# Attention on four quarter arrays: 64x64 tiles for scores and contexts, and the denominators in the score ring

## The chip, the cores and the metric

The kernel runs on one core of a Trainium2 chip. The metric is the device time of one execution in microseconds, the median of three runs. The engines meant below are TensorE (matrix products into PSUM, which has eight banks of 128 partitions x 512 float32), VectorE, ScalarE, GpSimd (POOL) and SyncE (SP, which issues DMAs).

## The reference

Two layers follow each other, all in float32. The first is attention over an image of 1024 channels and 32x32 pixels, so 1024 tokens, for four images. The second is a bottleneck of convolutions (1x1, 3x3, 1x1) with batch norms and a residual. The change touches only the attention:

```python
qkv = (x @ w_qkv.T + b_qkv).reshape(B, N, 3, nh, hd)      # nh 16 heads of hd 64, N 1024 tokens
q, k, v = (qkv[:, :, 0], qkv[:, :, 1], qkv[:, :, 2])
q = _rmsnorm(_apply_rope(q, cos, sin)); k = _rmsnorm(_apply_rope(k, cos, sin))
scores = jnp.einsum('bqhd,bkhd->bhqk', q, k) * hd ** (-0.5)
attn = jax.nn.softmax(scores, axis=-1)
ctx = jnp.einsum('bhqk,bkhd->bqhd', attn, v).reshape(B, N, inner)
out = _rmsnorm(ctx @ w_proj.T, norm_out_w) + residual
```

## The kernel before, in words

For each of the four images (b) the kernel projects q, k and v (`project2`, a Strassen-Winograd scheme of two levels), runs attention, and projects the contexts (y). Products with weights are cut so that TensorE works on 128x128 weights.

Attention (`attention`, L767) runs once for each half c of the queries (512 of them) and in it over eight pairs of heads hp. So an image has 16 pairs to go through, and the four images 64. In one pair:

- **Scores.** The 1024 keys are cut in eight blocks t of 128. For each block L787 makes two products, one for each head j of the pair. A head's 64 channels lie in one half of the partitions, so each product uses 64 rows and 128 columns of the array: two row tiles. Both go into a tile of two PSUM banks of the ring `sc`, which has three such tiles.
- **Probabilities.** ScalarE takes the exponential of both banks at once (L794) into `probs_`, which holds one pair's eight blocks.
- **Sums.** VectorE adds the blocks' probabilities into `d_` (L798, L800): seven additions of 128x1024 elements.
- **Contexts.** L808 multiplies the probabilities with v, 128 keys by the 64 channels of one head: two column tiles of 128x64, accumulated over the eight blocks in one PSUM bank, `cx`. ScalarE copies it to `q_all` (L813), over the queries, which are no longer needed.
- **Denominators.** After each second pair L841 sums `d_` over the partitions with a matrix of ones, as four column tiles of 128x32, into the bank `dn`. In the first half of the queries of images 1 to 3 (`fold`) GpSimd's DMAs fold four pairs' sums first, and one product for four pairs, `sum_of_eight` (L857), takes its place, also into `dn`. It is called two pairs later, between the scores and the contexts (L802). ScalarE copies `dn` at once (L863), or at the head of the next pair (`inverses`, L885, called by `late`); the copy goes to memory and back so that the reciprocal has few elements in a row, and `mean_of_v` (L761) multiplies the contexts some pairs later. For the last two pairs of an image there is no next pair: VectorE takes the reciprocal of `dn` itself (L891), after the y projection has begun.
- **What else is done in a pair**, after the contexts: `mean_of_v`; one waiting step (`next_waiting`), such as one head pair's rope of k (`turn`); and `extra` steps, in image 0 sums of weight blocks for the other projections (L392 to L395, L409 to L412), in the second half of image 3 the sums of the filters (L1086 to L1091).

`psum_for` (L189) closes PSUM's pools and opens those of the next stage: `o1` and `o2`, four banks each, for projections; `sc`, `cx` and `dn` for attention. Pools lie in PSUM in the order in which they are opened, and a tile of a new pool waits for the tile of the old pool that lay in the same bank (`reuse_waits="tile"`). In the y projection after attention, `start(0)` takes the first `o1` tile, `second(0)` the first `o2` tile, and VectorE forms four sums (`inner`, L450 to L454) before the reciprocal.

TensorE, VectorE, ScalarE and GpSimd are scheduled by hand here: each works its instructions off in the order in which the program issues them.

Of the kernel before, what the change touches and what calls it, by code (L numbers as in the profile page):

```python
# [13 lines left out]
ALU = mybir.AluOpType  # L14
# [4 lines left out]
P = 128  # L19
B, C, H, W = 4, 1024, 32, 32  # L20
N = H * W
NT = C // P
HD = 64
NHP = C // (2 * HD)
CH = 512
# [60 lines left out]
def program(ctx, tc, x, wblk, w2, w3, vecs, cos, sin, out, bad):  # L86


    nc = tc.nc
# [68 lines left out]
    with tc.tile_pool(name=f"st{u}", bufs=2) as st, ExitStack() as s:  # L158
# [30 lines left out]
        def psum_for(stage):  # L189

            open_pools.close()
            psum.clear()
            sizes = {
                "proj": [("o1", [P, CH], 4), ("o2", [P, CH], 4)],
                "att": [("sc", [P, 2, CH], 3), ("cx", [P, CH], 1), ("dn", [P, CH], 1)],
            }[stage]
            for name, shape, bufs in sizes:
                pool = open_pools.enter_context(
                    tc.tile_pool(name=f"{name}{u}{nc.next_id()}", bufs=bufs, space=PSUM, reuse_waits="tile")
                )  # L200
                psum[name] = (pool, shape)

        def bank(kind, name):
            pool, shape = psum[kind]
            return pool.tile(shape, F32, tag=kind, name=name)

        def temp(name):
            return tmp.tile([P, CH], F32, tag="tmp", name=name)
# [58 lines left out]
        def next_waiting():  # L267
            cost, step = waiting.popleft()
            spend(cost)
            step()  # L270
# [471 lines left out]
        def shifts(q_all, k_all, n, hp, c):  # L742

            rows = []
            for j in range(2):
                d = slice(j * HD, (j + 1) * HD)
                row = temp(f"row_{n}_{j}")[0:1, :]
                for t in range(CH // P):
                    sc = bank("sc", f"sm_{n}_{j}_{t}")
                    q = q_all[d, hp, c * CH + t * P : c * CH + (t + 1) * P]  # L750
                    for kh in range(N // CH):
                        nc.tensor.matmul(sc[:, kh], q, k_all[d, hp, half[kh]], start=True, stop=True)
                    m = acc.tile([P, 1], F32, tag="m", name=f"m_{n}_{j}_{t}")
                    nc.vector.tensor_reduce(m, sc.rearrange("p a k -> p (a k)"), AX.X, ALU.max, negate=True)
                    o = bank("dn", f"mt_{n}_{j}_{t}")
                    nc.tensor.matmul(o[0:1, :P], m, ident, start=True, stop=True)
                    nc.vector.tensor_copy(row[:, t * P : (t + 1) * P], o[0:1, :P])
                rows.append(row)
            return rows
# [7 lines left out]
        def attention(b, c, q_all, k_all, v, probs_, late, ready, extra, slow, steps_in_all, load_parts, fold):  # L767


            at = half[c]  # L770
            sums_ = []
            for hp in range(NHP):
                n = f"{b}_{c}_{hp}"
                if late:
                    late.pop(0)()
                rows = shifts(q_all, k_all, n, hp, c) if bad is None else None
                probs = []
                if fold and hp % 2 == 0:
                    d_ = fold[hp // 4][:, hp % 4 // 2 * 2 : hp % 4 // 2 * 2 + 2, :]
                else:  # L780
                    d_ = acc.tile([P, 2, CH], F32, tag="tot", name=f"den_{n}")
                for t in range(N // P):
                    p = probs_[:, t]
                    sc = bank("sc", f"sc_{n}_{t}")
                    for j in range(2):
                        d = slice(j * HD, (j + 1) * HD)
                        nc.tensor.matmul(  # L787
                            sc[:, j], k_all[d, hp, t * P : (t + 1) * P], q_all[d, hp, at],
                            start=True, stop=bad is not None,
                        )  # L790
                    if bad is None:
                        for j in range(2):
                            nc.tensor.matmul(sc[:, j], ones[0:1, :], rows[j], start=False, stop=True)
                    nc.scalar.activation(p, sc, AF.Exp)  # L794
                    if t == 3:
                        load_parts()
                    if t == 1:
                        nc.vector.tensor_tensor(d_, probs[0], p, ALU.add)  # L798
                    elif t > 1:
                        nc.vector.tensor_tensor(d_, d_, p, ALU.add)  # L800
                    probs.append(p)
                if eights and eights[0][0] <= c * NHP + hp:  # L802
                    eights.pop(0)[1]()
                o = bank("cx", f"cx_{n}")
                for t in range(N // P):
                    for j in range(2):
                        h0 = (2 * hp + j) * HD
                        nc.tensor.matmul(  # L808
                            o[j * HD : (j + 1) * HD, :], v[:, t, h0 : h0 + HD], probs[t][:, j],
                            start=(t == 0), stop=(t == N // P - 1),  # L810
                        )

                nc.scalar.copy(q_all[:, hp, at], o)  # L813
                sums_.append(d_)
                if hp % 2 == 1:
                    for r in ready:
                        mean_of_v(q_all, *r)
                    ready.clear()
                if fold:
                    halve(hp, d_, fold[hp // 4][:, hp % 4 // 2 * 2 : hp % 4 // 2 * 2 + 2, :])  # L820
                    if hp % 4 == 3:
                        eights.append((hp + 2, lambda n=n, hp=hp: sum_of_eight(b, n, hp, fold[hp // 4], ready)))
                if half_done and half_done[0][0] <= c * NHP + hp:
                    half_done.pop(0)[1]()
                if slow:
                    slow.pop(0)()

                if waiting:
                    next_waiting()
                slots = NCH * NHP - 1  # L830
                if extra and steps_in_all == 0 and hp > 0:
                    extra.pop(0)()
                for _ in range(len(extra) - -(-steps_in_all * max(slots - 1 - c * NHP - hp, 0) // slots) if steps_in_all else 0):
                    extra.pop(0)()
                if hp % 2 == 0 or fold:
                    continue
                dn = bank("dn", f"dn_{n}")
                for i, d_ in enumerate(sums_):
                    for j in range(2):
                        q = slice((2 * i + j) * QH, (2 * i + j + 1) * QH)  # L840
                        nc.tensor.matmul(dn[q, :], ones[:, :QH], d_[:, j], start=True, stop=True)  # L841
                sums_ = []
                late.append(lambda *a, n=n, hp=hp, dn=dn: inverses(b, c, hp, n, dn, ready))

        half_done, eights = [], []
        low, high = slice(0, P // 2), slice(P // 2, P)
# [9 lines left out]

        def sum_of_eight(b, n, hp, home, ready):  # L857

            dn = bank("dn", f"dn_{n}")
            for i in range(4):  # L860
                nc.tensor.matmul(dn[i * QH : (i + 1) * QH, :], halves, home[:, i, :], start=True, stop=True)
            r = temp(f"rec_{n}")
            nc.scalar.copy(r, dn)  # L863
            k = 2 * b * NCH * NHP + 2 * (hp - 3)
            few, rows = to_few(n, k, 8, r[:: QH // 2, :])

            def invert():
                nc.vector.reciprocal(few, few)
                nc.sync.dma_start(rows, few)
                for i in range(2):  # L870

                    at = [dens[k + 4 * i + q, :].partition_broadcast(QH) for q in (0, 2, 1, 3)]
                    spread(0, hp - 2 + 2 * i, n + f"_{i}", ready, at)

            half_done.append((hp + 3, invert))
# [288 lines left out]
        for b in range(B):  # L1164
            units = units_of(room)
            q_all = kv.tile([P, NT, N], F32, tag="q", name=f"q_{b}")
# [16 lines left out]
            k_all = kp.tile([P, NT, N], F32, tag="k", name=f"k_{b}")  # L1183
# [10 lines left out]
            v = room  # L1194
# [15 lines left out]
            def load_parts():  # L1210

                while todo and len(made) < 2:
                    made.append(todo.pop(0)(pieces, nc.sync))
# [279 lines left out]
        for b in range(B):  # L1493
# [34 lines left out]
            if b == 0 and bad is not None:  # L1528
                o = ps.tile([P, CH], F32, tag="mm", name="fit")
# [20 lines left out]
        for f in range(NT):  # L1550
# [8 lines left out]
            for i, k in order:  # L1559
                b, c = divmod(i, NCH)  # L1560
                nc.tensor.matmul(  # L1561
                    os[i], w3t[k][f // NH][:, f % NH, :], h2[b, k][:, half[c]],
                    start=(k == 0), stop=(k == NPT - 1),
# [11 lines left out]
            sc, sh = norms[f] = norm_of(stats, col("g3", f), col("be3", f), f"3_{f}")  # L1575
# [81 lines left out]
```

## Time and profile before

| | |
|---|---|
| time before, median of three runs | 2673.18 us (2672.54 to 2675.76) |
| profiled execution, first to last instruction (span) | 2669.7 us |
| median less span | 3.5 us |
| TensorE busy | 2643.4 us (99%) |
| VectorE busy | 2112.1 us (79%) |
| ScalarE busy | 1111.9 us (42%) |
| attention of images 0, 1, 2, 3, TensorE's stretches | 233.5, 230.4, 230.3, 230.9 us |
| mean granted TensorE clock | 0.998 |

The profiled execution's own time is taken as its span and the 3.5 us around it. A line of the page's groups gives the source line, the engine, the operation, the tiles written and read, the shape and the count; then busy time and mean duration in ns; then the engine's idle time before these instructions and what ended it. For a matmul, 64*128 means 64 rows and 128 columns of the array. Every float32 product is two matmuls, each with a weight load of its own (PEld). A line of a timeline gives start, duration, engine, source line, tiles, shape and count, and in brackets the idle time before it. A line of a table by stretches gives the stretch, its length, and busy time and instructions of TensorE, its weight loads, VectorE, ScalarE and GpSimd.

### The profile page before, as it was taken

How to read it: one execution, taken by the hardware profiler on the slowest of the kernel's cores; microseconds unless marked ns; L12 is line 12 of the kernel's file. 1: busy time of each engine (PE TensorE's matmuls, PEld its weight loads, DVE VectorE, ACT ScalarE, POOL GpSimd, SP SyncE). 2: the span in 40 equal slices, each digit the busy share in tenths (PEclk: the TensorE clock that was granted, in tenths of full speed). 3: DMA queues.
4: the chain of work that ended last, by engine and by line, in shares of the span. 5: the costliest groups of instructions: out<-in, count | busy, mean ns of one | idle time of the engine just before them, and what ended most of it. 6: DMA issues, size and time to landing. Idle time of an engine off the chain costs nothing.

```text
span 2669.7 us, 32558 instructions
## 1 busy us (share of the span) xinstructions
PE 2643.4 (99%) x11338; PEld 1650.7 (62%) x11338; DVE 2112.1 (79%) x2538; ACT 1111.9 (42%) x1549; POOL 470.6 (18%) x573
## 2 busy tenths in 40 slices
PE   9999999999999999999999999999999999999997
PEld 4448533488888333688886333888884335846843
DVE  5668899988787866788879667887988679877987
ACT  2222465423442555433343555233425654312266
POOL 2542233301011221200111222100111222010000
PEclk9999999999999999999999999999999999999999
DMA  7887676767667451456775541665774443583165
GB/s 277 292 255 215 197 244 206 236 211 250 169 181 215 83 102 41 157 152 222 191 196 148 92 77 33 211 203 178 191 214 87 82 100 115 172 279 103 64 236 206
DMA packets 255627, 459.22 MB, mean 172 GB/s; under 512 B 34912, under 2 KB 127632, under 8 KB 255456
## 3 DMA queue, kind: packets, MB, share of 16 engines
q1 hardware_dynamic: 210528, 306.73, 36.6%
q0 software_dynamic: 44928, 150.33, 22.3%
q8 instruction: 93, 1.52, 0.2%
q14 instruction: 78, 0.64, 0.1%
HBM read 327.43 MB, written 97.01 MB: 159 GB/s over the span
## 4 chain that ended last, share of the span: by engine, by line
PE 93%; DMA 3%; DVE 2%; issue 1%; ACT 1%; POOL 0%; SPq 0%; DVEq 0%; POOLq 0%; ACTq 0%
PE sc L787 16%; PE cx L808 16%; PE p_v L480 12%; PE p_y L485 12%; PE p_k L485 10%; PE p_q L485 9%; PE c L1561 4%; PE pa_q L303 2%; PE c2x L1422 2%; PE c L989 2%; PE c2y L1422 2%; PE pa_k L303 1%; PE c L948 1%; PE pc_q L303 1%; PE c1s L989 1%
## 5 line engine op out<-in xcount | busy, mean ns | idle before, releaser
L794 ACT ACTIVATE p<-sc 128x1024 f32<-128x1024 f32 x512 | 476.3, 1043 | 26.4 <-PE sc L787 24.3
L787 PE MATMUL sc<-q,k 64*128 64x512 f32 x2048 | 457.7, 596 | 0.0
L800 DVE TENSOR_TENSOR den<-den,p 128x1024 f32<-128x1024 f32 x312 | 384.9, 1234 | 33.6 <-DVE den L800 1.4
L787 PEld LDWEIGHTS sc<-q,k 64*128 64x128 f32 x2048 | 189.9, 186 | 265.2 <-issue 121.6
L808 PE MATMUL cx<-p,to 128*64 128x512 f32 x1536 | 340.2, 595 | 0.0
L808 PEld LDWEIGHTS cx<-p,to 128*64 128x64 f32 x1536 | 106.0, 137 | 228.7 <-issue 228.7
L480 PE MATMUL p_v<-w_v,x 128*128 128x256 f32 x928 | 209.9, 379 | 0.0
L485 PE MATMUL p_y<-q,w_y 128*128 128x256 f32 x928 | 209.8, 379 | 0.0
L765 POOL TENSOR_SCALAR q<-q,vec 128x512 f32<-128x512 f32 x64 | 128.1, 2010 | 384.7 <-DVE q L764 376.5
L485 PEld LDWEIGHTS p_y<-q,w_y 128*128 128x128 f32 x928 | 176.0, 190 | 27.1 <-issue 3.4
L480 PEld LDWEIGHTS p_v<-w_v,x 128*128 128x128 f32 x928 | 176.1, 190 | 25.2 <-DVE x L451 0.9
L813 ACT COPY q<-cx 128x512 f32<-128x512 f32 x64 | 37.6, 587 | 360.0 <-PE cx L808 360.0
L798 DVE TENSOR_TENSOR den<-p 128x1024 f32<-128x1024 f32 x52 | 64.6, 1243 | 120.4 <-ACT p L794 120.4
L485 PE MATMUL p_q<-to,w_q 128*128 128x256 f32 x672 | 152.2, 379 | 0.0
L485 PE MATMUL p_k<-to,w_k 128*128 128x256 f32 x672 | 152.2, 379 | 0.0
L485 PEld LDWEIGHTS p_q<-to,w_q 128*128 128x128 f32 x672 | 127.4, 190 | 18.4 <-issue 1.2
L485 PEld LDWEIGHTS p_k<-to,w_k 128*128 128x128 f32 x672 | 127.4, 190 | 18.4 <-issue 1.2
L808 PE MATMUL cx<-p,rq 128*64 128x512 f32 x512 | 113.4, 595 | 0.0
L1561 PE MATMUL c<-h,w 128*128 128x512 f32 x256 | 110.3, 592 | 0.5 <-ACT h L1464 0.5
L800 DVE TENSOR_TENSOR den_T<-den_T,p 128x1024 f32<-128x1024 f32 x72 | 88.2, 1225 | 7.5
L727 POOL DMA_DIRECT2D k<-ks x64 | 57.9, 1097 | 190.7 <-ACT p L794 71.1
L485 PE MATMUL p_y<-to,w_y 128*128 128x256 f32 x384 | 90.4, 380 | 1.1 <-DMA w_y<-wdf 1.0
(490 smaller groups left out, 4266.0 us busy)
## 6 DMA issues: line engine op xcount, KB each, us to landing
w_v<-wd2f SPq DMA_DIRECT2D x112, 256.0 KB, 3.2
w_y<-wd2f SPq DMA_DIRECT2D x112, 256.0 KB, 2.8
w_q<-wd2f SPq DMA_DIRECT2D x84, 256.0 KB, 2.8
w_k<-wd2f SPq DMA_DIRECT2D x84, 256.0 KB, 2.6
wd2f<-w_pre POOLq DMA_DIRECT2D x68, 256.0 KB, 3.9
x<-in_x_dram SPq DMA_DIRECT2D x64, 256.0 KB, 5.9
q<-qs POOLq DMA_DIRECT2D x64, 256.0 KB, 5.5
k<-ks POOLq DMA_DIRECT2D x64, 256.0 KB, 4.5
```

The source lines that it names most:

```text
L303: nc.tensor.matmul(o, w[:, i, :], r(i), start=first and i == 0, stop=last and i == NH - 1, skip_group_check=True,)
L480: nc.tensor.matmul(o[:, q].rearrange("p (g f) -> p g f", g=2), r[:, i, q * P : (q + 1) * P], wt[:, :, i, :], skip_group_check=True, **at,)
L485: nc.tensor.matmul(o[:, q], wt[:, q, i, :], r[:, i, :], skip_group_check=True, **at)
L765: nc.gpsimd.tensor_scalar(cx, cx, col("bv", hp), None, ALU.add)
L787: nc.tensor.matmul(sc[:, j], k_all[d, hp, t * P : (t + 1) * P], q_all[d, hp, at], start=True, stop=bad is not None,)
L794: nc.scalar.activation(p, sc, AF.Exp)
L798: nc.vector.tensor_tensor(d_, probs[0], p, ALU.add)
L800: nc.vector.tensor_tensor(d_, d_, p, ALU.add)
L808: nc.tensor.matmul(o[j * HD : (j + 1) * HD, :], v[:, t, h0 : h0 + HD], probs[t][:, j], start=(t == 0), stop=(t == N // P - 1),)
L989: nc.tensor.matmul(o, wt[:, i, :], rows(i), start=first and i == 0, stop=last and i == NH - 1, skip_group_check=True,)
L1422: nc.tensor.matmul(o[:, r * TR * TC : (r + 1) * TR * TC], uw[2 * h + r, j][:, i * PL + f * P : i * PL + (f + 1) * P], vt[b, i][:, 2 * h + ...
L1561: nc.tensor.matmul(os[i], w3t[k][f // NH][:, f % NH, :], h2[b, k][:, half[c]], start=(k == 0), stop=(k == NPT - 1),)
```

## The change

Scores are made by four products a block instead of two: the 128 keys are cut in two halves, so each product uses a tile of 64 rows and 64 columns. Contexts are made by four products a block as well: the 128 keys are cut in two halves of the partitions, each half accumulates in a PSUM bank of its own, and `cx` has two banks. ScalarE copies the first as before; VectorE adds the second to it, after the pair's other steps. The pool `dn` is gone: denominators take half of a tile of the ring `sc`. The call of `sum_of_eight` moves from between scores and contexts to behind that addition.

```diff
-                "att": [("sc", [P, 2, CH], 3), ("cx", [P, CH], 1), ("dn", [P, CH], 1)],
+                "att": [("sc", [P, 2, CH], 3), ("cx", [P, 2, CH], 1)],
...
-            sums_ = []
+            sums_, contexts = [], []
...
-                    for j in range(2):
-                        d = slice(j * HD, (j + 1) * HD)
-                        nc.tensor.matmul(
-                            sc[:, j], k_all[d, hp, t * P : (t + 1) * P], q_all[d, hp, at],
-                            start=True, stop=bad is not None,
-                        )
+                    for keys in (low, high):
+                        for j, d in enumerate((low, high)):
+                            nc.tensor.matmul(
+                                sc[keys, j], k_all[d, hp, t * P + keys.start : t * P + keys.stop], q_all[d, hp, at],
+                                start=True, stop=bad is not None,
+                            )
...
-                if eights and eights[0][0] <= c * NHP + hp:
-                    eights.pop(0)[1]()
                 o = bank("cx", f"cx_{n}")
                 for t in range(N // P):
                     for j in range(2):
                         h0 = (2 * hp + j) * HD
-                        nc.tensor.matmul(
-                            o[j * HD : (j + 1) * HD, :], v[:, t, h0 : h0 + HD], probs[t][:, j],
-                            start=(t == 0), stop=(t == N // P - 1),
-                        )
-
-                nc.scalar.copy(q_all[:, hp, at], o)
+                        for i, keys in enumerate((low, high)):
+                            nc.tensor.matmul(
+                                o[j * HD : (j + 1) * HD, i], v[keys, t, h0 : h0 + HD], probs[t][keys, j],
+                                start=(t == 0), stop=(t == N // P - 1),
+                            )
+
+                nc.scalar.copy(q_all[:, hp, at], o[:, 0])
+                contexts.append((q_all[:, hp, at], o[:, 1]))
...
+                for cx, other in contexts:
+                    nc.vector.tensor_tensor(cx, cx, other, ALU.add)
+                contexts.clear()
+                if eights and eights[0][0] <= c * NHP + hp:
+                    eights.pop(0)[1]()
                 if hp % 2 == 0 or fold:
                     continue
-                dn = bank("dn", f"dn_{n}")
+                dn = bank("sc", f"dn_{n}")[:, 0]
...
         def sum_of_eight(b, n, hp, home, ready):
-            dn = bank("dn", f"dn_{n}")
+            dn = bank("sc", f"dn_{n}")[:, 0]
```

The second program (`bad is None`), which runs only where a denominator leaves its bounds, gets the same tiles; it does not run on these inputs.

More of the change, by code (lines that the diff above doesn't have):

```diff
@@ L754, in shifts @@
                     nc.vector.tensor_reduce(m, sc.rearrange("p a k -> p (a k)"), AX.X, ALU.max, negate=True)
-                    o = bank("dn", f"mt_{n}_{j}_{t}")
+                    o = bank("sc", f"mt_{n}_{j}_{t}")[:, 0]
                     nc.tensor.matmul(o[0:1, :P], m, ident, start=True, stop=True)
```

## The prediction

> **What bounds the kernel now.** I read the page's busy line and chain first, then its groups, then the waits, then TensorE's and VectorE's timelines of attention.
>
> ```profile
> PE 2643.4 (99%) x11338; PEld 1650.7 (62%) x11338; DVE 2112.1 (79%) x2538; ACT 1111.9 (42%) x1549; POOL 470.6 (18%) x573
> ...
> PE 93%; DMA 3%; DVE 2%; issue 1%; ACT 1%; POOL 0%; SPq 0%; DVEq 0%; POOLq 0%; ACTq 0%
> PE sc L787 16%; PE cx L808 16%; PE p_v L480 12%; PE p_y L485 12%; PE p_k L485 10%; PE p_q L485 9%; PE c L1561 4%; PE pa_q L303 2%; PE c2x L1422 2%; PE c L989 2%; PE c2y L1422 2%; PE pa_k L303 1%; PE c L948 1%; PE pc_q L303 1%; PE c1s L989 1%
> ...
> L787 PE MATMUL sc<-q,k 64*128 64x512 f32 x2048 | 457.7, 596 | 0.0
> L800 DVE TENSOR_TENSOR den<-den,p 128x1024 f32<-128x1024 f32 x312 | 384.9, 1234 | 33.6 <-DVE den L800 1.4
> ```
>
> TensorE is the path: scores and contexts are 16% each. 2048 score matmuls of 596 ns would be 1221 us in a row, but the chain gives them 427: two row tiles run side by side. So both products already fill the array. The timeline of TensorE over one pair of heads, then a denominator:
>
> ```profile
> 907.59 0.60 PE L808 MATMUL cx<-p,to 128*64 128x512 f32 x2
> 908.12 7.14 PE L787 MATMUL sc<-q,k 64*128 64x512 f32 x32
> 915.19 7.09 PE L808 MATMUL cx<-p,to 128*64 128x512 f32 x32
> 922.21 1.13 PE L787 MATMUL sc<-q,k 64*128 64x512 f32 x4
> ...
> 346.12 1.06 PE L841 MATMUL dn<-den,ones 128*32 128x512 f32 x8
> ```
>
> A pair of heads takes 922.21 - 908.12 = 14.09 us. By the single start times, matmuls start two at a time (6 ns apart, one per tile) every 0.429 us; only at the changes of shape is it more: 0.519 and then 0.480 from scores to contexts (0.141 over), 0.529 and then 0.534 from contexts to scores (0.205 over). 32 x 0.429 = 13.73 and 0.346 make the 14.08. The last line shows four column tiles at once: eight matmuls in 1.06 us.
>
> VectorE, by stretch (attention of images 0 and 1), and the end of image 0's attention:
>
> ```profile
> 287.60:521.10 233.50, 233.43 (x1081) 84.21 (x1080) 213.13 (x223) 133.24 (x151) 76.41 (x105) 1.00 0.67 217
> 865.80:1096.20 230.40, 230.40 (x1065) 83.76 (x1064) 165.07 (x145) 131.85 (x149) 51.32 (x48) 1.00 0.35 69
> ...
> 521.11 1.06 PE L841 MATMUL dn<-den,ones 128*32 128x512 f32 x8
> 522.11 3.72 PE L485 MATMUL p_y<-q,w_y 128*128 128x256 f32 x16
> 525.01 3.35 DVE L891 RECIPROCAL rec<-dn 128x512 f32<-128x512 f32 x1
> 528.41 0.92 PE L485 MATMUL p_y<-y,w_y 128*128 128x256 f32 x3 [0.86 <-DVE rec L891]
> ```
>
> VectorE is busy 213 of 233.5 us in image 0, and between its 223 instructions lie some 0.06 to 0.1 us each: it has almost no slack there, 65 us in image 1. And the last line is what I build on: a PSUM bank makes the next stage wait. The last denominator sits in the `dn` bank until the 3.35 us reciprocal has read it, and the output projection, whose second `o2` tile is that bank (7), waits.
>
> [...] 0.141 and 0.205 us at each change of shape, nothing at a change of tile. [...] The forecast takes the drain's size and VectorE's load from the trace.
>
> **The change, part by part.**
>
> *Four 64x64 tiles.* Twice the matmuls, a quarter of the array each. The trace shows two row tiles at once (scores), two and four column tiles at once, not two by two. If four run, a step stays 0.429 us and the stream costs nothing more or less. Weight loads (137 ns for 64 columns, 187 for 128) stay under it. Bounds: nothing, and twice the time if only two run (rival 2). I take nothing.
>
> *No change of shape.* A pair of heads without a denominator goes from 14.08 to 13.73. One with a denominator keeps two changes (64x64 to 128x32 and back), so it only saves scores to contexts: 15.08 to 14.94. In images 1 to 3: eleven pairs x 0.346, the one with both sums at its end (pair 9 of 16) 0.29, three with one sum and the last pair 0.14 each: 4.65 us an image.
>
> *The added VectorE instruction.* 128x512 from SBUF and PSUM: 64 of them. The nearest row, the projection's addition from PSUM (L506), has 0.685 us, with a pitch of 0.61 back to back; I take 0.65, bounds 0.61 and 0.72. It stands behind all of a pair's VectorE work (sums of exponentials, rope or weight steps), waits for ScalarE's copy of the other half (0.59 us after the contexts), and ahead of the next pair's sums. In images 1 and 2 the slack hides it: VectorE waits 2 to 7 us a pair for the exponentials from the third pair on. Queued behind it are the next pair's sums, which are due 3.15 us after the next scores' start, 2.3 us after the addition's end; for the sums wait the exponentials (they overwrite the probabilities) and the denominators. The next contexts' first matmul, which needs the one context buffer back, comes 6.9 us after the last contexts. Without that slack each addition costs its 0.65.
>
> In image 0 nothing hides it. I take each pair's VectorE work from the timeline, from one first sum to the next less waits (14.41, 12.04, 14.79, 14.12, 14.79, 13.91, 12.16, 16.54, 12.16, 16.53, 12.16, 13.9, 14.75, 13.9, 14.95), and three rules: the first sum follows the pair's scores by 3.15 us; odd pairs' denominators need the last sum, 9.35 after the first; contexts need the addition before. With the old values this gives the last pair's scores at 507.0, as measured (507.03), and 7 us of waits. With 0.65 more a pair and TensorE's 13.73/14.94 the waits are used up by the seventh pair, and VectorE sets the pace: last scores at 509.1, its first sum at 515.1 (511.9 before), last denominator at 524.45 instead of 521.11.
>
> *Denominators in the score ring.* During attention nothing: a denominator takes a slot long free, ScalarE copies it before the next exponentials, and the third following scores need it 1.7 us on, after a copy of 0.6. At the end of an image it matters. In the program of before the score ring's slots are banks 0-1, 4-5, 2-3 in turn; the projection's first `o1` tile is bank 0, the first `o2` tile bank 4. Image 0 takes 128 scores + 8 denominators: the last is the 136th, slot 0, hence bank 0. Images 1 to 3 take 128 + 2 + 4: the 134th, slot 1, bank 4. So the very first projection tile (image 0) or the second (images 1 to 3) waits for the reciprocal. And this comes later: VectorE's queue is addition, four sums (L450 to L454), reciprocal, and the addition waits for ScalarE's copy.
>
> - Images 1, 2 (image 1's times): denominator 1096.21, copy done 1096.91, addition to 1097.65, four sums 2.82, reciprocal 3.35: 1103.8. The second tile would start 1.8 us after 1097.20, at 1099.0: it waits 4.85. Less 4.65 saved: +0.2 each.
> - Image 3: the same 4.85, less the 0.23 its weight load waited before, plus 1.8 because the filter steps load VectorE (it idles under 0.5 us a pair at its end) and the last denominator then waits for the sums; less 4.5: +1.9.
> - Image 0: VectorE runs without a gap from 511.87 to the reciprocal's end 528.36, 16.49 us; now 515.1 + 16.49 + 0.65 = 532.2. The first tile starts there instead of at 522.11, +10.1, less the 0.86 waited before: +9.2.
>
> *The eighths' sums moved* (L802 to the end of the pair): nothing is on the path of their result for several pairs; they save one pair of drains in pair 9, counted. *Instructions:* 8192 more on TensorE; its queue has issued weight load and matmul 31 ns apart after a wait (249.38, 249.41); needed are 16 in 0.858 us, 54 ns each. I take nothing.
>
> Sum: 9.2 + 0.2 + 0.2 + 1.9 = +11.5 us on the profiled span of 2669.7: 2681.2. The median stands 3.5 above the span: **2684.7**. Its own range is 2679 to 2694 (additions at 0.61 or 0.72, a denominator's changes of shape 0.2 dearer, image 3 with or without its 1.8).
>
> **Rivals.**
>
> 1. *No collision of banks* (faster): if the last denominator's slot is not the projection's first or second tile, image 0 costs 3.3 - 0.86 = +2.5, images 1 and 2 -4.65 each, image 3 -2.9: -9.7, 2663.5. It decides wherever the reciprocal ends before its bank is asked for. For: the drains, 64 x 0.346 = 22 us, are real. Against: the wait of 0.86 us shows that such a tile waits, and the count of slots. Chance 0.20.
> 2. *TensorE does not carry four tiles at that rate.* If only two run: 64 x 13.73 = +879. [...] Against: four column tiles at once, and 31 ns above. Chance 0.08.
> 3. *Changing the tile costs what changing the shape does:* the 14 us saved in images 1 to 3 are gone: +25, 2699. Against: nothing is seen between row tiles. Chance 0.07.
> 4. *Half the collision:* it holds in images 1 to 3 or in image 0 alone, or the tiles get another bank: 2668 to 2678, no measurable change. Chance 0.10.
>
> Forecast 0.55. This measurement tells about 0.2% (5.3 us) from no change. Slower: 0.55 + 0.08 + 0.07 = 0.70; same 0.10; faster 0.20. The range, 2661 to 2701, leaves out rival 2 and edges of the others.
>
> **What would show it.** Right: pairs of 13.73 us in image 1 (14.09 before), four matmuls per 0.429 us; image 0's pairs no shorter, VectorE there without waits from the seventh pair on; the first product after image 0's attention waiting 7 us for the reciprocal, the second one some 5 us after the others. Wrong: pairs of 14.1 or over in image 1 (rivals 2, 3), or a projection that starts without a wait (rival 1).

## The result, and the profile after

The changed kernel takes 2703.1 us (median of four runs, 2701.9 to 2704.5) against 2673.8 us beside it (2672.5 to 2675.8): a ratio of 1.0108, 95% interval 1.0094 to 1.0123. It is slower, as forecast, but by 29.3 us, not by 11.5; the time lies above the forecast's range. The profiled span grew by 32.7 us, from 2669.7 to 2702.4. Where these 32.7 us lie, from the first starts of each pair's scores in TensorE's timeline (us):

| stretch | before | after | difference | forecast |
|---|---|---|---|---|
| ahead of image 0's attention | 287.57 | 288.27 | +0.7 | 0 |
| image 0: first to last pair's scores | 219.46 | 236.46 | **+17.0** | **+2.1** |
| from there to image 1's first scores | 358.73 | 368.80 | +10.1 | +7.1 |
| image 1: first to last pair's scores | 216.36 | 211.64 | -4.7 | -4.65 |
| from there to image 2's first scores | 356.75 | 362.36 | +5.6 | +4.85 |
| image 2: first to last pair's scores | 216.36 | 211.64 | -4.7 | -4.65 |
| from there to image 3's first scores | 357.06 | 364.04 | +7.0 | +4.85 |
| image 3: first to last pair's scores | 216.55 | 211.70 | -4.9 | -4.5 |
| from there to the end | 440.81 | 447.44 | +6.6 | +6.4 |

The page of the changed kernel, busy line and groups:

```profile
PE 2642.7 (98%) x15434; PEld 1634.4 (60%) x15434; DVE 2152.2 (80%) x2602; ACT 1112.0 (41%) x1549; POOL 470.0 (17%) x573
...
L787 PE MATMUL sc<-q,k 64*64 64x512 f32 x4096 | 453.1, 591 | 0.0
L485 PE MATMUL p_y<-q,w_y 128*128 128x256 f32 x928 | 217.2, 388 | 21.6 <-issue 21.6
L807 PE MATMUL cx<-p,rq 64*64 64x512 f32 x1024 | 117.7, 610 | 9.3 <-DVE q L836 9.3
```

TensorE is busy for the same 2643 us and idle for 33 us more. Twice the score matmuls fit into 453 us, where 458 were needed before. Two groups of TensorE's now have long idle times ahead of them: the output projection (21.6 us in front of four products) and image 0's contexts (`rq` is image 0's tile), 9.3 us behind the added instruction L836. TensorE's timeline, first over one pair of heads of image 1, then at the ends of image 0's, image 1's and image 2's attention:

```profile
934.89 7.05 PE L787 MATMUL sc<-q,k 64*64 64x512 f32 x64
941.76 7.05 PE L807 MATMUL cx<-p,to 64*64 64x512 f32 x64
948.62 7.05 PE L787 MATMUL sc<-q,k 64*64 64x512 f32 x64
...
549.27 5.58 PE L485 MATMUL p_y<-q,w_y 128*128 128x256 f32 x16 [7.08 <-issue]
...
1119.02 1.06 PE L846 MATMUL dn<-den,ones 128*32 128x512 f32 x8
1120.02 1.99 PE L485 MATMUL p_y<-q,w_y 128*128 128x256 f32 x8
1126.67 3.58 PE L485 MATMUL p_y<-q,w_y 128*128 128x256 f32 x8 [4.67 <-issue]
1130.09 3.62 PE L485 MATMUL p_y<-y,w_y 128*128 128x256 f32 x16
...
1700.67 3.75 PE L485 MATMUL p_y<-q,w_y 128*128 128x256 f32 x8 [4.66 <-issue]
1704.21 4.91 PE L485 MATMUL p_y<-y,w_y 128*128 128x256 f32 x16
```

The pair is 948.62 - 934.89 = 13.73 us, the forecast's number. The first product after image 0's attention waits 7.08 us, the second of image 1 4.67 (image 2 4.66, image 3 5.16). These are the two collisions of banks. But in image 1 the eight matmuls behind the wait take 3.58 us where the eight before it took 1.99, and in image 2 the next sixteen are slow as well (4.91 us against image 1's 3.62). The table by stretches says why; its last three columns are TensorE's granted clock, the DMA share and GB/s:

```profile
288.30:539.00 250.70, 238.30 (x2105) 79.10 (x2104) 219.79 (x236) 133.25 (x151) 77.10 (x105) 0.98 0.62 199
893.50:1119.50 226.00, 226.00 (x2097) 78.17 (x2096) 174.20 (x160) 132.39 (x150) 51.85 (x48) 1.00 0.36 71
...
430.20:433.60 3.40, 0.00 (x0) 0.00 (x0) 2.57 (x5) 1.41 (x2) 0.12 (x1) 1.00 0.03 2
433.70:434.50 0.80, 0.00 (x0) 0.00 (x0) 0.80 (x3) 0.00 (x0) 0.80 (x2) 0.50 0.45 144
434.60:440.40 5.80, 5.80 (x28) 1.75 (x32) 5.38 (x5) 0.00 (x0) 1.02 (x2) 0.50 0.90 312
...
549.20:553.00 3.80, 3.73 (x9) 3.04 (x10) 3.70 (x4) 0.00 (x0) 0.00 (x0) 0.50 0.59 195
1126.70:1130.00 3.30, 3.30 (x8) 2.68 (x9) 3.19 (x3) 0.00 (x0) 0.00 (x0) 0.51 0.72 241
```

The first two rows are the attention of images 0 and 1: in image 0 TensorE now lacks 12 us and VectorE is idle for 31 (20 before), though it has 6.7 us more to do. The others show the clock. It falls to half within a stand (between 433.6 and 433.7 us in the rows shown, while no product runs) or, at 471.2 us, 1.2 us behind one of 3.61, and then runs products at half speed for a while: for 3.8, 3.3, 6.1 and 2.8 us behind the stands of the four projections, and for 5.9 and 3.4 us at two stands in image 0's attention. Half of these times is what it costs: 7.9 us in the projections (by the products 5.58 - 3.72 in image 0; 3.58, 3.75 and 3.35 less 1.97 in images 1 to 3; and 4.91 - 3.62 in image 2), 4.7 in image 0's attention. These 12.6 us count as busy time; the shape changes saved 14.3 in images 1 to 3, so TensorE's busy time hardly moved. The last section has the times at which the clock changed.

In image 0 two pairs are worst. VectorE, SP and TensorE of the changed kernel around one of them:

```profile
415.42 5.64 SPq L383 DMA_DIRECT2D w_pre<-in_wblk_dram  x4
421.16 1.99 SPq L383 DMA_DIRECT2D w_pre<-wdf  x4
423.25 0.50 SPq L883 DMA_DIRECT2D densf<-rec  x1
427.84 0.34 SPq L887 DMA_DIRECT2D few<-densf  x1
430.93 0.25 DVE L904 RECIPROCAL few<-few 128x16 f32<-128x16 f32 x1 [5.72 <-DMA few<-densf]
433.82 0.68 DVE L836 TENSOR_TENSOR q<-q,cx 128x512 f32<-128x512 f32 x1
434.56 10.01 PE L807 MATMUL cx<-p,rq 64*64 64x512 f32 x64 [4.45 <-DVE q L836]
```

And the same denominators' trip in the kernel before:

```profile
410.06 0.38 SPq L383 DMA_DIRECT2D w_pre<-in_wblk_dram  x1
410.53 0.50 SPq L878 DMA_DIRECT2D densf<-rec  x1
411.13 3.31 SPq L383 DMA_DIRECT2D w_pre<-in_wblk_dram  x3
415.09 0.34 SPq L882 DMA_DIRECT2D few<-densf  x1
```

Before, ScalarE's copy of the denominators ended at 406.2 and SP wrote them out at 410.53, behind one weight load. After, the copy ended at 409.8 and SP wrote them at 423.25, behind eight loads, which themselves waited for GpSimd to write back VectorE's weight sums (from 413.0 on; over image 0 and the start of its projection SP waits 78.6 us for these writes, 66.1 before). So `few` arrives late, VectorE stands in the small reciprocal L904, its four weight sums and the added L836 come behind it, and the next contexts, which need the bank that L836 reads, stand for 4.45 us and then run at half clock. VectorE's waits in image 0's attention, kernel before, then after (line waited in, releaser, us, times, longest):

```profile
DVE den L798 <- ACT p L794: 5.4, 6, 2.0
DVE few L899 <- DMA few<-densf: 2.3, 3, 0.9
```

```profile
DVE few L904 <- DMA few<-densf: 16.5, 6, 5.7
DVE den L798 <- ACT p L794: 0.8, 1, 0.8
```

Both are for 287 to 525 us; up to the end of image 0's attention in the changed kernel the trip's waits come to 17.9 us, in seven pairs. The waits for exponentials are used up, as forecast. The waits for the trip did not go; they grew from 2.3 to over 16 us.

### The profile page after: what moved, and what is told of

It is laid out like the page before. It is cut to its first block, busy times and chain, and to the rows that moved or that the text cites. A ratio compares the mean times of both kernels' runs of the same rounds, so it can differ in the third digit from the quotient of the medians.

```text
span 2702.4 us, 40776 instructions
## 1 busy us (share of the span) xinstructions
PE 2642.7 (98%) x15434; PEld 1634.4 (60%) x15434; DVE 2152.2 (80%) x2602; ACT 1112.0 (41%) x1549; POOL 470.0 (17%) x573
## 5 line engine op out<-in xcount | busy, mean ns | idle before, releaser
L787 PE MATMUL sc<-q,k 64*64 64x512 f32 x4096 | 453.1, 591 | 0.0
L807 PE MATMUL cx<-p,to 64*64 64x512 f32 x3072 | 338.2, 589 | 0.0
L787 PEld LDWEIGHTS sc<-q,k 64*64 64x64 f32 x4096 | 151.0, 132 | 291.7 <-ACT p L794 143.5
L807 PEld LDWEIGHTS cx<-p,to 64*64 64x64 f32 x3072 | 117.4, 133 | 212.2 <-issue 211.9
L485 PE MATMUL p_y<-q,w_y 128*128 128x256 f32 x928 | 217.2, 388 | 21.6 <-issue 21.6
L807 PE MATMUL cx<-p,rq 64*64 64x512 f32 x1024 | 117.7, 610 | 9.3 <-DVE q L836 9.3
L807 PEld LDWEIGHTS cx<-p,rq 64*64 64x64 f32 x1024 | 39.5, 137 | 85.8 <-issue 69.9
```

The costliest lines, as they stand in the source:

```text
L485: nc.tensor.matmul(o[:, q], wt[:, q, i, :], r[:, i, :], skip_group_check=True, **at)
L787: nc.tensor.matmul(sc[keys, j], k_all[d, hp, t * P + keys.start : t * P + keys.stop], q_all[d, hp, at], start=True, stop=bad is not None,)
L807: nc.tensor.matmul(o[j * HD : (j + 1) * HD, i], v[keys, t, h0 : h0 + HD], probs[t][keys, j], start=(t == 0), stop=(t == N // P - 1),)
```

## The experiments

Theory 1: image 0's excess comes from the denominators' trip, which stands in SP's queue, so that L904 stops VectorE with the added instruction queued behind it. Theory 2: VectorE simply has more to do than the forecast took, and the wait shows up wherever it can. In the projections: the banks are all of it, or something else is late beneath them. Times are medians; the kernel before was 2672.7 to 2673.5 beside them. "Pairs" is image 0's first to last scores in the profiled execution (219.5 before, 236.5 after). In three versions that leave image 0's pairs and SP's order there as in the changed kernel, the pairs came out at 230.3, 231.4 and 233.1: that excess is 11 to 17 us over four profiled executions, one of each.

**1. Image 0's contexts as before.**

```diff
+                        if b == 0:
+                            nc.tensor.matmul(
+                                o[j * HD : (j + 1) * HD, 0], v[:, t, h0 : h0 + HD], probs[t][:, j],
+                                start=(t == 0), stop=(t == N // P - 1),
+                            )
+                            continue
...
+                if b > 0:
+                    contexts.append((q_all[:, hp, at], o[:, 1]))
```

> The changed kernel with the contexts of image 0 alone as before: two 128x64 tiles in one bank, and no added VectorE instruction; images 1 to 3, scores and denominators stay changed. If the added instruction is what stretches image 0 (either theory of the way): the sixteen pairs of image 0 are back within 0 to 5 us of the kernel before (219.5 us from the first pair's last scores to the last pair's, 236.5 in the changed kernel): 2686 to 2691. If it is the denominators in the score ring or the order of SP's loads that the new order brought: 230 us or more there, 2697 or more.

Measured: 2683.0, pairs 219.96. The scores there are four tiles and the denominators lie in the ring, so neither is what stretches image 0. The edit takes away the contexts' four tiles together with the added instruction; those tiles cost nothing in images 1 to 3 (pairs of 13.73 us), which leaves the instruction. SP's order is back too:

```profile
408.84 0.38 SPq L383 DMA_DIRECT2D w_pre<-in_wblk_dram  x1
409.31 0.50 SPq L890 DMA_DIRECT2D densf<-rec  x1
409.90 4.46 SPq L383 DMA_DIRECT2D w_pre<-in_wblk_dram  x3
414.45 0.44 SPq L894 DMA_DIRECT2D few<-densf  x1
```

So the order in which the framework puts SP's transfers depends here on instructions that SP does not issue.

**2. The small reciprocal one pair later, everywhere.** In `inverses`:

```diff
-            half_done.append((0, invert))
+            half_done.append((c * NHP + hp + 2, invert))
```

> The changed kernel with one number: the short reciprocal of the denominators (L904) is written one pair of heads later in VectorE's order, so that the trip copy, densf, few has some 14 us more. Theory 1 (in image 0 VectorE stands still in L904 for a trip that waits in SP's queue behind the weight loads): the waits of L904 (18 us in seven pairs) go, the waits of TensorE for the added instruction (cx <- q, 9.3 us) go or fall under 2, and image 0's pairs fall by 10 to 17 us: 2686 to 2693. Theory 2 (VectorE is simply loaded more by the added instructions, and the waits in L904 would turn up at another of its instructions): 2700 to 2703. Images 1 to 3 are unchanged in both.

Measured: 2694.8, just above the range, pairs 218.8 (-17.7), no wait of TensorE for L836 left. In this version the last but one trip comes after the projection's first sums have read its contexts, so part of the projection is made from undivided contexts and the result is wrong; image 0's pairs lie ahead of that. It gave back some 9 us in the stretches after attention, where `p_y` waited another 7.4 us for its weights; the next run leaves that trip where it was.

**3. The same in image 0 alone, without its last but one trip.**

```diff
-            half_done.append((0, invert))
+            last = (c, hp) == (NCH - 1, NHP - 3)
+            half_done.append((c * NHP + hp + 2 if b == 0 and not last else 0, invert))
```

> The changed kernel with the short reciprocal of the denominators one pair later in image 0 alone, and there not for the last but one trip (c = 1, hp = 5). Images 1 to 3 keep the changed kernel's order. Theory 1 (the trip stands behind SP's weight loads, and VectorE stands in L904 for it): image 0 runs from the first pair's last scores to the last pair's in 218 to 222 us as with the reciprocal later everywhere (218.8), not 236.5, and nothing is given back in images 1 to 3: 2703.1 - 17 = 2686, at most 2688. If the 9 us that the version with all images moved gave back come from image 0's order itself: 2694. Theory 2 (plain load): 2700 or more.

Measured: 2689.0 (ratio 1.0067, 1.0050 to 1.0084), pairs 219.1. VectorE's waits in the same stretch:

```profile
DVE few L904 <- DMA few<-densf: 0.9, 1, 0.9
```

Theory 2 falls: with all sixteen additions in place and VectorE's work unchanged, image 0's pairs are as short as before the change, once the trip has time. SP's order moved with this edit too: the write of the trip shown above left at 416.72 us, behind five loads. That it is 1 us above 2688 fits the projection's first product, which now waits 9.0 us instead of 7.1.

**4. Nothing moved on VectorE, but the trip's two transfers on GpSimd's queue (image 0).**

```diff
-            nc.sync.dma_start(dens[k : k + rows_, :], r)
+            trip = nc.gpsimd if b == 0 else nc.sync
+            trip.dma_start(dens[k : k + rows_, :], r)
...
-            nc.sync.dma_start(few, rows)
+            trip.dma_start(few, rows)
```

> The changed kernel with the two transfers of the denominators' trip (densf <- rec and few <- densf) issued by GpSimd instead of SP in image 0; nothing is moved on VectorE and the added instructions stay. Theory 1 in its exact form (the trip is late because it stands in SP's queue behind weight pieces that wait for buffers): the waits of L904 in image 0 fall from 18 us to under 6, and its pairs from 236.5 us to 222 to 226: 2690 to 2694. Theory 1 in a weaker form (any slack cures it, the queue is not the cause; or GpSimd's own writes of the sums stand ahead of the trip in the same way): 2698 or more. Theory 2 (plain load): unchanged, 2703.

Measured: 2695.0, pairs 227.8. VectorE's waits, then GpSimd's timeline at the trip shown above:

```profile
DVE few L905 <- DMA few<-densf: 8.0, 4, 3.7
```

```profile
410.71 4.30 POOL L397 DMA_DIRECT2D wd2f<-w_pre  x8
415.00 0.57 POOL L884 DMA_DIRECT2D densf<-rec  x1
422.12 0.58 POOL L888 DMA_DIRECT2D few<-densf  x1 [6.55 <-DMA densf<-rec]
```

Half of it, between the two expectations: the median fell by 8.1 us, where experiment 3 gained 14.1. The pairs fell by 8.7 against the changed kernel's execution, but only by 2.5 against the shortest of the four named above. So SP's queue is a part of the delay, about half by the medians; no run gives its share exactly. The trip stays late on GpSimd: there it stands behind eight writes, and its own write takes 6.55 us to land.

**5. The last denominator off the colliding banks.** Tiny products take ring slots ahead of it, so that it lies in banks 2 and 3.

```diff
+                if (c, hp) == (NCH - 1, NHP - 1):
+                    for i in range(1 + (b == 0)):
+                        nc.tensor.matmul(bank("sc", f"skip_{n}_{i}")[0:1, 0, :P], ones[:, :1], ones, start=True, stop=True)
                 dn = bank("sc", f"dn_{n}")[:, 0]
```

> The changed kernel with one tiny product (one column of ones, 128 wide) into the next ring slot ahead of the last denominator of each image, two in image 0, so that this denominator lies in banks 2 and 3, which the projection wants only with its third o1 tile. Theory of the bank collision: the waits 'PE p_y L485 <- issue: 21.6' go. Theory of the clock on top of it: the 6.9 us by which the products right behind those waits were longer go too, since TensorE no longer stands still: 2703.1 - 21.6 - 6.9 + about 1 for the five tiny products = 2675.6. If the half clock came from something else than the waits: 2682.5. Rival, the waits only hide another one (VectorE's sums of the projection come late as well): above 2690. Image 0's pairs stay at +17.

Measured: 2699.3, a clear miss. The waits at the banks are gone, and others of nearly the same length stand in their place. TensorE's waits (one line of the view), then TensorE and SP after image 1's attention:

```profile
PE p_y L485 <- DMA w_y<-in_wblk_dram: 18.5, 4, 4.9
```

```profile
1129.78 5.36 PE L485 MATMUL p_y<-q,w_y 128*128 128x256 f32 x16 [4.45 <-DMA w_y<-in_wblk_dram]
...
1113.66 4.84 SPq L215 DMA_DIRECT2D x<-in_x_dram  x10
1121.11 0.51 SPq L900 DMA_DIRECT2D densf<-rec  x1
1121.66 4.99 SPq L917 DMA_DIRECT2D inv<-rec  x8
1126.75 0.53 SPq L383 DMA_DIRECT2D w_y<-in_wblk_dram  x1
```

The third product's weights stand behind the nine transfers that wait for the last reciprocal. The changed kernel has the same order there (ten loads of x, then these nine, then the weights). The kernel before has four loads of x, then these weights, then the nine. So under the collision lay a second loss, again made by SP's order; the collision hid it. Taking the collision away alone gains 3.8 us by the medians; in the profiled execution only 2.0 of its gain lie behind attention, and 3.4 in image 0's pairs, which the edit does not touch.

**6. The last reciprocal ahead of the projection's first sums.**

```diff
-            after(0.1, late.pop(0))
+            late.pop(0)()
```

> The changed kernel with the last reciprocal of each image ahead of the first sums of the projection on VectorE, not behind them. The slot stays in the colliding bank. Bank collision: TensorE's stand in images 1 to 3 falls from 4.8 to about 1.9 us each, in image 0 from 7.1 to about 4.3. Theory that the clock is halved only after a long stand: in images 1 to 3 the products behind it take 1.9 us for eight again (they took 3.4 to 3.75), in image 0 they stay slow: 2703.1 - 11.6 - 5.0 = 2686.5. If any stand halves the clock: 2691.5. Rival, the sums that are now later hold TensorE up instead: 2700 or more.

Measured: 2684.6 (ratio 1.0045, 1.0028 to 1.0062): -18.5. The reciprocal releases both the bank and SP. TensorE and its stretches in image 1, then image 0's stretch:

```profile
1114.15 1.97 PE L485 MATMUL p_y<-q,w_y 128*128 128x256 f32 x8 [1.82 <-issue]
```

```profile
1114.10:1118.00 3.90, 3.85 (x18) 3.44 (x19) 3.69 (x6) 0.13 (x1) 0.00 (x0) 1.00 0.63 198
540.50:544.00 3.50, 3.48 (x8) 2.85 (x9) 3.40 (x5) 0.00 (x0) 0.00 (x0) 0.50 0.63 205
```

After a stand of 1.82 us the clock is full and the eight matmuls take 1.97 us, which took 3.58 behind the changed kernel's 4.67; after image 0's 4.07 us it is 0.50. So the half clock here came with the stand, not with the products behind it. The stands became 11.7 us shorter in all, and 6.1 us of half clock went: 17.8 against the medians' 18.5. The profiled execution saves 3.7 to 5.6 us after each image's attention from image 1 on (rests of 358.6, 358.5 and 443.1), 4.3 after image 0's; 5.0 more lie in image 0's pairs, which the edit does not touch.

**7. Trying to clear SP's queue.** Experiment 5, with the nine transfers behind the last reciprocal on GpSimd:

```diff
-                nc.sync.dma_start(dens[k : k + 4, :], r[::QH, :])
+                nc.gpsimd.dma_start(dens[k : k + 4, :], r[::QH, :])
...
-                    nc.sync.dma_start(w[j * QH : (j + 1) * QH, half[i]], rows[2 * i + j // 2])
+                    queue = nc.gpsimd if (c, hp) == (NCH - 1, NHP - 1) else nc.sync
+                    queue.dma_start(w[j * QH : (j + 1) * QH, half[i]], rows[2 * i + j // 2])
```

> The changed kernel with the last denominator moved off the colliding banks as before (tiny products), and in addition the nine transfers behind the last reciprocal (denominators out, inverses to their 128 rows) issued by GpSimd instead of SP, so that the weights of the third product no longer stand behind them. Theory of two stands one under the other (bank, then weights in SP's queue): the waits of p_y for w_y (18.5 us in the version with the slots alone) go, and the halved clock behind them (about 6 us): 2675 to 2678. Rival, the transfers are now late on GpSimd's queue, or the weights wait for something else: 2690 or more.

Measured: 2697.2, a miss. Fourteen loads of the next image (256 KB each) moved into the gap on SP, and the weights are still late:

```profile
1110.46 8.07 SPq L215 DMA_DIRECT2D x<-in_x_dram  x14
1118.93 0.38 SPq L383 DMA_DIRECT2D w_y<-in_wblk_dram  x1
...
1125.59 4.64 PE L485 MATMUL p_y<-q,w_y 128*128 128x256 f32 x13 [3.46 <-DMA w_y<-in_wblk_dram]
```

Then the loads of x on GpSimd's queue too (`load_x(b + 1, c, (i,), nc.gpsimd)`), with image 0's small reciprocal later as in 3:

> The changed kernel with image 0's reciprocal one pair later, the last denominator off the colliding banks, its nine transfers and the sixteen loads of the next image both on GpSimd's queue, so that SP carries only the weights of the projection; the last reciprocal stays behind the first sums. Theory that the weights of the third product were late because 10 to 14 loads of x and the reciprocal's nine transfers stood ahead of them on SP: no wait of p_y for w_y is left, and the shape changes' gain of some 15 us shows: 2657 to 2663. Rival, GpSimd's queue now makes the inverses or the next image late (means of v wait, or sums of x): 2668 or more.

Measured: 2681.6. The third product's wait is gone in images 0 to 2, and a later one has come, 3 us an image for `w_y<-wdf`, while GpSimd's loads of x are running, which now start 34 us after the last pair's first scores in image 1 (14 us in the version before it). The time is the rival's, but the wait is not the one it named: the weights are late again, on SP. The same move without the transfers on GpSimd and with the reciprocal ahead of the sums:

> The version with all repairs and the transfers of the last reciprocal on SP, with the loads of the next image moved to GpSimd's queue. The reciprocal stays ahead of the first sums, so the second product's wait of 1.3 us an image for those sums (3.6 in image 0, with the half clock behind it) stays: 2664 to 2669 if the loads of x were what made the weights late, 2670 as before if they were not.

Measured: 2687.0, worse than its counterpart with x on SP (2670.2, below): it too waits 9.2 us for `w_y<-wdf`. That is outside both expectations; moving the loads of x did not bring the weights forward there. That the two sets of transfers get in each other's way at the DMA engines is my reading; no run separates it from the order of the queues.

**8. The repairs together**: 3, 5 and 6, with the nine transfers on GpSimd:

> The changed kernel with all the repairs: reciprocal of image 0 one pair later, last denominator off the colliding banks, its transfers on GpSimd's queue, and the last reciprocal of each image ahead of the first sums. Theory that image 0's trip, the bank and the weights behind it are the whole loss: the gain of the shape changes (4.7 us in each of images 1 to 3, and about 1 in image 0) is left: 2673 - 15 = 2658, up to 2664 if a wait of a microsecond an image stays. If a loss remains that none of the three explains: above 2670.

and with them on SP:

> As the version with all repairs, but the transfers behind the last reciprocal stay on SP. The reciprocal ahead of the sums lets SP issue them some 3 us earlier. If SP's order (weights of the third product behind them) still costs: a wait of 1 to 3 us an image with its halved clock, 2664 to 2672; if the earlier reciprocal is enough: within 2 us of the version on GpSimd's queue.

Measured: 2672.8 (ratio 1.0001, 0.9992 to 1.0010) and 2670.2 (0.9992, 0.9983 to 1.0001). The pairs are all repaired (219.2 in image 0; 211.6, 211.8 and 211.7 in images 1 to 3), but 2658 was missed. Of the shape changes' 14 us most is still given back after attention, in the version on SP: 364.9, 357.9, 359.0 and 444.1 against 358.7, 356.8, 357.1 and 440.8 of the kernel before. The second product now waits for the first sums, which stand behind the reciprocal: 1.3 to 1.7 us an image, 3.6 in image 0. These 7.8 us and the half clock behind image 0's wait (1.7) are most of the 12.6 given back. Last, the version with the transfers on SP, with the last pair of each image as before the change (two tiles, no addition):

```diff
+                        if (c, hp) == (NCH - 1, NHP - 1):
+                            nc.tensor.matmul(
+                                o[j * HD : (j + 1) * HD, 0], v[:, t, h0 : h0 + HD], probs[t][:, j],
+                                start=(t == 0), stop=(t == N // P - 1),
+                            )
+                            continue
...
+                if (c, hp) != (NCH - 1, NHP - 1):
+                    contexts.append((q_all[:, hp, at], o[:, 1]))
```

> The version with image 0's reciprocal one pair later, the last denominator off the colliding banks and the last reciprocal ahead of the first sums (2670.2), with the contexts of the last pair of each image as before the change: two 128x64 tiles in one bank and no added instruction, since there ScalarE's copy and the add stand between the last context and the reciprocal. Theory that the second product's remaining wait (1.3 us an image, 3.6 in image 0 with a half clock behind it) comes from this reciprocal and add ahead of the sums: both sums and reciprocal start 1 to 1.8 us sooner, the wait goes in images 1 to 3 and falls to about 2 in image 0, less 0.3 us an image for two shape changes: 2664 to 2667. Rival, the weights on SP are late next: 2669 or more.

Measured: 2669.7 against 2673.1 (ratio 0.9988, 0.9981 to 0.9995). It is the one version faster than the kernel before, by 0.12%, less than the 0.2% that I took as the bound of what can be told. TensorE after image 1's attention:

```profile
1102.95 3.69 PE L485 MATMUL p_y<-y,w_y 128*128 128x256 f32 x16 [1.24 <-issue]
1111.71 3.69 PE L485 MATMUL p_y<-q,w_y 128*128 128x256 f32 x16 [1.61 <-DMA w_y<-in_wblk_dram]
```

The expected gain did not come: the wait for the sums stayed at 1.24 us, and the weights are late right behind it, as the rival had it.

## Why the prediction was right in direction and wrong in size

- *Four 64x64 tiles cost nothing*: right. Pairs of 13.73 us in images 1 to 3; rival 2 falls. Why each half of the keys has a context bank of its own is not shown: no run puts both in one.
- *No change of shape, 4.65 us an image*: right, 4.7, 4.7 and 4.9. Rival 3 falls. (What the prediction calls a drain is the 0.141 and 0.205 us measured at a change of shape; what the array does in that time is not shown.)
- *The added instruction, 0.65 us, hidden in images 1 to 3*: right; 62 of the 64 took 0.67 to 0.69.
- *Bank 0 in image 0, bank 4 in the others*: right, and rivals 1 and 4 fall. I had 4.85 us for images 1 to 3, against 4.67, 4.66 and 5.16; in image 0 the product waited 7.08, as "what would show it" had it.
- *"The waits are used up by the seventh pair, and VectorE sets the pace: last scores at 509.1"*: **this step failed**, and it is most of the miss. The last scores began at 524.7. The recurrence let every wait of VectorE shrink as work was added. Of the 8.2 us of waits before, 0.5 lay between two sums, 5.4 were for exponentials and did shrink, to 0.8; the 2.3 us in the small reciprocal were for a transfer whose own start depends on VectorE's weight sums through GpSimd and SP, and these grew to 16.5. No rule of the recurrence held that transfer's start; it was taken to stay where it was. The edit added the instruction on VectorE, and SP's order changed with it. The term was +2.1 and measured +17.0 (+11 to +17 over executions). Experiments 1 and 3 show the instruction and the trip as its two halves; experiment 4 shows SP's queue as part of the delay.
- *A stand costs its own length*: this was left unsaid, and is the second step that failed: the half clock behind a stand was put at nothing. It costs 7.9 us behind the four stands of the projections, and 4.7 of image 0's 17 (pairs 9 and 11). Experiment 6 brings three of these stands down to 1.8 to 2.1 us, and the half clock behind them goes.
- *Where a stall goes, what is late next*: I asked this for VectorE and not for SP. Beneath the collision lay weights for which TensorE waits 18.5 us in sum, hidden as long as the collision stands. This did not make the prediction wrong, but rival 1's 2663.5 would not have come true: without the collision the kernel takes 2699.3, and image 0's longer pairs are only 13.6 us of it.
- The sum: 2.1 + 7.1 in image 0 became 27.1; the other three images 2.3 became about 5; and 0.7 came ahead of attention, a stretch that no edit touches and that took 286.6 to 289.4 us in the profiles. The spans differ by 32.7 us and the medians by 29.3, in part because the 3.5 us that were laid around a span were 1.8 in the changed kernel (2704.2 less 2702.4).

## What to carry to other kernels

Before adding an instruction to an engine that is nearly full, sort its waits by what ends them. Here the waits for a faster engine were slack and absorbed the work (5.4 us to 0.8); the waits for a transfer that starts from this engine's own output were a loop and grew (2.3 to 16.5). Where a framework orders a queue, an edit on one engine can reorder the DMA issues of another, so read that queue's order before and after. Where a wait is to be removed, look for the next transfer in line: here a bank's wait of 4.7 us covered a weight's wait of 4.4. And add to a stand of TensorE what a half clock takes behind it: here 12.6 us, over a third of the 32.7.

## What the runs showed of the hardware

- Four 64x64 tiles of float32 matmuls ran at the pace of two 64x128 ones: four starts every 0.429 us, at 4096 scores and as many contexts. In the pair shown above, 64 score matmuls start from 934.89 to 941.76 us and 64 of the contexts from there to 948.62, which leaves nothing over at the two changes between them.
- In the changed kernel's trace the granted clock was 1.00 or 0.50. Between 10.4 us and the last product it fell six times, at 433.64, 471.18, 546.28, 1126.54, 1699.98 and 2276.84 us, and stayed at 0.50 for 6.83, 3.41, 6.83, 3.41, 6.83 and 3.41 us. These twelve changes lie whole multiples of 3.413 us apart; why is not shown. In the 3.41 us ahead of five of these falls no matmul ran; ahead of the one at 471.18 us TensorE stood for 2.16 of them.
- The length of a stand alone did not decide what followed. In experiment 7 a stand of 2.93 us was followed by eight matmuls in 3.54 us (image 1 of the second version) and another of 2.93 us by eight in 1.97 (image 2 of the third); one of 3.12 us, in the third version's image 0, was followed by eight in 1.97 too.
- The same image 0 program took 230.3 to 236.5 us from its first to its last pair's scores in four profiled executions of versions that differ only behind it. In the six versions in which the trip has time (experiments 3, 7 and 8) it took 218.7 to 219.6. That fits the loop through the DMA queues as the source of the spread; each version was profiled once.
